# Head-by-head exponentials with bias and running sum in a decoder layer's self-attention softmax

## The chip, the cores and the metric

The kernel is one launch on one core of a Trainium2 chip. The metric is the device time of one execution in microseconds (us). All arithmetic is in 32-bit floats.

## The reference, cut to what matters

The reference is one decoder layer: each of three blocks (self-attention, cross-attention to a context, and a mixture-of-experts feed-forward) is applied to a layer-normed input and added to the residual. Only the first block is touched here. There are 8 sequences of 112 tokens, width 512, 16 heads of 128.

```python
k = jnp.einsum('ihd,bpd->biph', W_K, x)          # x is already layer-normed
q = jnp.einsum('ihd,bpd->biph', W_Q, x)
v = jnp.einsum('ihd,bpd->biph', W_V, x)
scores = jnp.einsum('biph,biqh->biqp', k, q)
mask = jnp.tril(jnp.ones((pos, pos), dtype=x.dtype))
masked = scores * mask - jnp.float32(10000000000.0) * (1.0 - mask)
attn = jax.nn.softmax(masked / jnp.sqrt(jnp.float32(d_head)), axis=-1)
z = jnp.einsum('biqp,biph->biqh', attn, v)
z_flat = jnp.transpose(z, (0, 2, 1, 3)).reshape(b, pos, -1)
out = jnp.einsum('df,bqf->bqd', W_O, z_flat)
```

The softmax needs, for each sequence, head and query, the largest score of the row, the exponentials of the scaled differences to it, their sum, and the division by that sum.

## The kernel before, in words

The 896 tokens lie in 7 tiles of 128 rows. Rows 0 to 111 of tile t hold sequence t+1; sequence 0 is cut into seven pieces of 16 tokens which fill rows 112 to 127 of all tiles. The program names this with `seq(ap, b)`.

Self-attention runs over four groups (`g`) of four heads each (`GH = 4`). A group has three stages.

1. **Queries and keys.** `pair_of_heads` makes `qT` and `kT` for the group, with a scheme of sums that saves matmuls (lines 249 to 282; TensorE line 261). GpSimd forms the weight sums.
2. **Softmax and values.** A loop over sequences 1, 0, 2, 3, 4 calls `softmax(b)` and then `value(i)`. `value(i)` (line 338) is eight matmuls for one token tile; ScalarE copies them out (line 342), and a DMA on SP's queue (line 343, `v<-v`) carries the 16 rows of sequence 0 into a tile of their own, `vals[0]`. Values 5 and 6 follow without a softmax.
3. **Weighted sums and output projection.** `turn(b)` transposes the softmax weights of four heads on TensorE (line 218) and ScalarE copies them to `sT` (line 220); `weighted(b)` multiplies them with the values (line 226) and VectorE copies the result to `zT` (line 233); `project_o(t)` multiplies `zT` with the output weights (line 348) and VectorE adds it to the residual (line 355). The remaining softmaxes 5, 6 and 7 are called in this loop, in iterations b = 1, 2 and 3, four sequences ahead of their use.

One call of `softmax(b)` works on four heads at once, a tile `s` of 112 rows by 4 x 112 scores. TensorE writes the scores to PSUM (line 191). VectorE adds the mask while it copies them to SBUF (line 199), takes the row maxima `mx` (line 206) and subtracts them (line 207). ScalarE takes the exponential of the whole tile in one instruction, with the factor 1/sqrt(128) as its scale (line 208). VectorE sums the rows to `sm` (line 210) and inverts the sums (line 211). GpSimd multiplies (line 212).

Four PSUM buffers, the pool `sc`, are shared in turn by the scores `s`, the transposes `pT` and the sums `z`: a new one waits until the one four allocations earlier has been read out. The tile framework orders the instructions of each engine when it builds the program, and puts in the waits; each engine then works its queue strictly in order. On TensorE the third stage of a group begins pT(1), pT(0), s(5), pT(2), z(1), s(6), pT(3), z(2), z(0), s(7), pT(4), z(3), where s(5) are the scores of sequence 5, pT(1) the transpose of sequence 1 and z(0) the weighted sum of sequence 0. The first projection, called o(0) below, comes next in the first three groups, and needs zT(0) and zT(1).

Of the kernel before, what the change touches and what calls it, by code (L numbers as in the profile page):

```python
# [17 lines left out]
AF = mybir.ActivationFunctionType  # L18
ALU = mybir.AluOpType
AX = mybir.AxisListType  # L20

P = 128
B, S, D = 8, 112, 512
# [5 lines left out]
H, DH = 16, 128  # L29
GH = 4  # L30
# [29 lines left out]
def seq(ap, b):  # L60

    if b:
        return ap[..., (b - 1) * P : (b - 1) * P + S]
    axes = " ".join("abcd"[: len(ap.shape) - 1])
    return ap.rearrange(f"{axes} (t i) -> {axes} t i", t=TT)[..., S:]


def like_seq(ap, b):

    if b:  # L70
        return ap
    axes = " ".join("abcd"[: len(ap.shape) - 1])
    return ap.rearrange(f"{axes} (t i) -> {axes} t i", t=TT)
# [3 lines left out]
def decoder_layer(  # L77
    ctx: ExitStack, tc: tile.TileContext, x, ctxT, wqk, wv_all, wo, wx, wgate, wsgu, wsd, wegu, wed_a, wed_b, consts, out
):
    nc = tc.nc  # L80
# [15 lines left out]
    mask = cst[:S, C_MASK : C_MASK + S]  # L96
# [20 lines left out]
    def psum(pool, name):  # L117
        return pool.tile([P, 512], F32, tag=pool.name, name=name)

    def load_w(pool, src, name):  # L120
        t = pool.tile([P, 4, 512], F32, tag="w", name=name)
        nc.sync.dma_start(out=t, in_=src)
        return t
# [53 lines left out]
    with ExitStack() as sa:  # L177
# [10 lines left out]
        def softmax(b, qT, kT, q0):  # L188
            ps = psum(sc, "s")
            for h in range(GH):  # L190
                nc.tensor.matmul(  # L191
                    like_seq(ps[:S, h * S : (h + 1) * S], b),
                    qT[:, h, (b - 1) * P : (b - 1) * P + S] if b else q0[:, h, :],
                    seq(kT[:, h, :], b),
                    start=True,
                    stop=True,
                )
            s = sp.tile([S, GH, S], F32, tag="s", name="s", bufs=5)
            nc.vector.tensor_tensor(
                s,  # L200
                ps[:S, : GH * S].rearrange("q (h p) -> q h p", h=GH),
                mask[:, None, :].to_broadcast([S, GH, S]),
                ALU.add,
            )
            mx = sp.tile([S, GH], F32, tag="mx", name="mx")
            nc.vector.tensor_reduce(mx, s, AX.X, ALU.max)
            nc.vector.tensor_tensor(s, s, mx[:, :, None].to_broadcast([S, GH, S]), ALU.subtract)  # L207
            nc.scalar.activation(s, s, AF.Exp, scale=float(DH) ** -0.5)  # L208
            sm = sp.tile([S, GH], F32, tag="sm", name="sm")
            nc.vector.tensor_reduce(sm, s, AX.X, ALU.add)  # L210
            nc.vector.reciprocal(sm, sm)  # L211
            nc.gpsimd.tensor_tensor(s, s, sm[:, :, None].to_broadcast([S, GH, S]), ALU.mult)  # L212
            return s
# [9 lines left out]
        def weighted(b, sT, v, zT):  # L223
            pz = psum(sc, "z")
            for h in range(GH):
                nc.tensor.matmul(  # L226
                    pz[:, h * S : (h + 1) * S],
                    v[:S, h * DH : (h + 1) * DH],
                    sT[:, h, :],
                    start=True,  # L230
                    stop=True,
                )
            nc.vector.tensor_copy(
                seq(zT, b), like_seq(pz[:, : GH * S].rearrange("p (h q) -> p h q", h=GH), b)
            )
# [48 lines left out]
        for g in range(NG):  # L284
            if g == 0:

                wq, wk = (wpool.tile([P, 4, 512], F32, tag="w", name=f"w{i}_0") for i in range(2))
                for h in range(GH):
                    for i, w in enumerate((wq, wk)):
                        nc.sync.dma_start(out=w[:, h, :], in_=wqk[i, g][:, h, :])  # L290
            else:
                wq, wk = (load_w(wpool, wqk[i, g], f"w{i}_{g}") for i in range(2))
            wv = load_w(wvpool, wv_all[g], f"w2_{g}")
            wog = wvpool.tile([P, 4, 512], F32, tag="w", name=f"wo_{g}")
            load = nc.sync.dma_start(out=wog, in_=wo[g])
            if g == 0:
                first_weights = load.ins
                with tc.issue_after(first_weights):
                    nc.sync.dma_start(out=gw, in_=wgate)
                    nc.sync.dma_start(  # L300
                        out=slots.rearrange("(j p) d -> p j d", p=P),
                        in_=zeros[:, None, :].to_broadcast([P, NS, D]),
                    )
            qT = qkp.tile([P, GH, NT], F32, tag="qT", name="qT")
            kT = qkp.tile([P, GH, NT], F32, tag="kT", name="kT")
            zT = zp.tile([P, GH, NT], F32, tag="zT", name="zT")
            for h in range(0, GH, 2):
                for w, dst, pool in ((wq, qT, mm), (wk, kT, sc)):
                    if g == 0 and h == 0 and dst is qT:

                        for half in range(2):
                            cols = bass.ds(half * HALF, HALF)
                            for i in range(2):
                                ps = psum(mm, "qk")
                                for c in range(ND):
                                    nc.tensor.matmul(
                                        ps[:, :HALF],
                                        w[:, i, c * P : (c + 1) * P],
                                        xn1[:, c, cols],
                                        start=(c == 0),  # L320
                                        stop=(c == ND - 1),
                                    )
                                nc.scalar.copy(dst[:, i, cols], ps[:, :HALF])
                            if half == 0:
                                rs1 = norm1(4, TT)
                                for t in range(4, TT):
                                    ln_apply(mv1, rs1[t - 4], t, xn1)
                                token_sums()
                        continue
                    pair_of_heads(w, h, dst, pool)  # L330
            soft, turned, vals = {}, {}, {}
            vals[0] = v0p.tile([S, GH * DH], F32, tag="v0", name="v0")

            def value(t):

                ps = psum(mm, "v")
                for c in range(ND):
                    nc.tensor.matmul(  # L338
                        ps, xn1[:, c, t * P : (t + 1) * P], wv[:, c, :], start=(c == 0), stop=(c == ND - 1)
                    )  # L340
                vals[t + 1] = vp.tile([P, GH * DH], F32, tag="v", name="v")
                nc.scalar.copy(vals[t + 1], ps)
                nc.sync.dma_start(out=vals[0][t * SP : (t + 1) * SP, :], in_=vals[t + 1][S:, :])

            def project_o(t):
                ps = psum(mm, "o")
                for h in range(GH):
                    nc.tensor.matmul(  # L348
                        ps,
                        zT[:, h, t * P : (t + 1) * P],  # L350
                        wog[:, h, :],
                        start=(h == 0),
                        stop=(h == GH - 1),
                    )
                nc.vector.tensor_tensor(xs[t], ps, xs[t], ALU.add)  # L355
                if g == NG - 1:
                    ln_stats(mv2, t)


            q0 = vp.tile([P, GH, S], F32, tag="q0", name="q0", bufs=1)  # L360
            nc.gpsimd.tensor_copy(like_seq(q0, 0), seq(qT, 0))
            for i, b in enumerate((1, 0, 2, 3, 4)):
                soft[b] = softmax(b, qT, kT, q0)
                value(i)
            for i in (5, 6):
                value(i)
            for b in (1, 0):
                turned[b] = turn(soft.pop(b))
            for b in range(1, B):
                if b + 4 < B:  # L370
                    soft[b + 4] = softmax(b + 4, qT, kT, q0)
                if b + 1 < B:
                    turned[b + 1] = turn(soft.pop(b + 1))
                weighted(b, turned.pop(b), vals.pop(b), zT)
                if b == 2:
                    weighted(0, turned.pop(0), vals.pop(0), zT)
                elif b > 2:
                    project_o(b - 3)
            project_o(TT - 2)
            project_o(TT - 1)  # L380
# [347 lines left out]
    with ExitStack() as ff:  # L728
# [335 lines left out]
        h = {}  # L1064
# [109 lines left out]
```

## Time and profile before

| what | value |
|---|---|
| median of 3 runs | 1017.53 us (1015.96 to 1018.1) |
| the profiled execution's own time | 1016.08 us |
| its span, first to last instruction | 1014.3 us |
| TensorE's granted clock | 1.00 |
| busy: TensorE matmul, VectorE, ScalarE, GpSimd | 98%, 40%, 27%, 25% of the span |
| self-attention, four groups | about 14 to 448 us of the span |
| cross-attention; feed-forward | to about 760 us; to the end |

A busy share is the time in which an engine had an instruction under way. In the views, PE is TensorE's matmul, PEld its weight load, DVE is VectorE, ACT is ScalarE, POOL is GpSimd, SP the engine that issues most DMAs. An arrow `s<-qT,kT` names the tile written and the tiles read. Brackets in the timeline give the idle time of the engine before an instruction and what ended it; that name is inferred from semaphore events, and where an instruction has several waits it is the one that came last by the profile.

### The profile page before, as it was taken

Reading aid. Unit: us, or ns where it says so; the run is one execution under the profiler, and the core shown is the slowest. Engines: PE = TensorE matmul, PEld = TensorE weight load, DVE = VectorE, ACT = ScalarE, POOL = GpSimd, SP = SyncE. Lnnn points to the kernel's source line nnn. Section 1 sums busy time; section 2 is a strip of 40 time slices with the busy share of each in tenths; the row PEclk is TensorE's granted clock in tenths of the full one; section 3 lists DMA queues with packets and bytes.
Section 4 is the critical chain, followed back from the end, with each engine's and each line's share of the span. In section 5 each row is a group of like instructions: output and inputs, shape, how many; then the busy total and the mean of one; then the engine's idle time right before and its main releaser. Section 6 shows DMA issues by size and latency. Waiting matters only on the chain.

```text
span 1014.3 us, 14761 instructions
## 1 busy us (share of the span) xinstructions
PE 991.4 (98%) x5732; PEld 527.0 (52%) x5732; DVE 401.9 (40%) x769; ACT 276.9 (27%) x522; POOL 246.6 (24%) x269
## 2 busy tenths in 40 slices
PE   5999999999999999999999999999999999999998
PEld 3556555654556455645455555565565544444433
DVE  4345224532345225545432444343425333333315
ACT  2122011310022012213354555455543111221100
POOL 4341034103411122112533223330205600000023
PEclk9999999999999999999999999999999999999999
DMA  9521002101201111000000001000209738777765
GB/s 343 201 83 47 5 38 84 50 1 42 79 16 41 42 41 47 5 1 0 31 32 1 32 32 32 2 32 2 83 3 377 297 112 258 235 235 236 216 190 171
DMA packets 31093, 95.66 MB, mean 94 GB/s; under 512 B 3888, under 2 KB 5808, under 8 KB 27440
## 3 DMA queue, kind: packets, MB, share of 16 engines
q1 hardware_dynamic: 25968, 82.11, 24.0%
q0 software_dynamic: 2320, 7.63, 2.3%
q10 hardware_dynamic: 2736, 4.98, 1.6%
q8 instruction: 46, 0.75, 0.3%
q14 instruction: 23, 0.19, 0.1%
HBM read 78.85 MB, written 14.94 MB: 92 GB/s over the span
## 4 chain that ended last, share of the span: by engine, by line
PE 90%; issue 3%; DVE 3%; DMA 2%; POOL 1%; ACT 1%; SPq 0%; DVEq 0%; POOLq 0%; ACTq 0%
PE qk L261 16%; PE o L348 10%; PE v L338 10%; PE kv L482 9%; PE gu L744 5%; PE xs L577 5%; PE gate L980 4%; PE y L1002 4%; PE up L980 4%; PE pv L602 4%; PE ys L1028 3%; PE k L423 3%; PE xv L423 3%; PE z L226 2%; PE s L191 2%
## 5 line engine op out<-in xcount | busy, mean ns | idle before, releaser
L585 ACT ACTIVATE e<-xs 125x448 f32<-125x448 f32 x192 | 88.4, 545 | 72.7 <-PE xs L577 72.7
L338 PE MATMUL v<-w,xn 128*128 128x512 f32 x224 | 100.4, 594 | 0.0
L348 PE MATMUL o<-wo,zT 128*128 128x512 f32 x224 | 99.8, 594 | 0.0
L261 PE MATMUL qk<-xc,wc 128*128 128x448 f32 x180 | 70.1, 539 | 0.0
L348 PEld LDWEIGHTS o<-wo,zT 128*128 128x128 f32 x224 | 41.0, 190 | 44.0 <-issue 44.0
L338 PEld LDWEIGHTS v<-w,xn 128*128 128x128 f32 x224 | 40.7, 190 | 42.1 <-issue 41.1
L212 POOL TENSOR_TENSOR s<-s,sm 112x448 f32<-112x448 f32 x32 | 30.1, 941 | 129.2 <-DVE sm L211 100.5
L1013 POOL DMA_INDIRECT got<-routed,at x14 | 14.7, 1054 | 173.4 <-DMA routed<-y 169.1
L980 PE MATMUL gate<-wex,xT 128*64 x144 | 55.3, 466 | 0.5 <-ACT xT L945 0.5
L744 PE MATMUL gu<-xn,sw 128*128 128x448 f32 x144 | 55.5, 541 | 0.0
L980 PE MATMUL up<-wex,xT 128*64 x144 | 54.3, 459 | 0.0
L577 PE MATMUL xs<-qT,kT 32*125 32x224 f32 x768 | 50.4, 373 | 1.5 <-DVE qT L540 1.5
L930 DVE COPY xn<-wex 128x704 f32 x60 | 31.2, 524 | 51.5 <-PE up L980 51.5
L261 PEld LDWEIGHTS qk<-xc,wc 128*128 128x128 f32 x180 | 34.2, 190 | 33.4 <-issue 32.3
L261 PE MATMUL qk<-xn,w 128*128 128x448 f32 x120 | 50.2, 539 | 0.0
L577 PEld LDWEIGHTS xs<-qT,kT 32*125 32x125 f32 x768 | 33.2, 181 | 32.5 <-issue 28.5
L1002 PE MATMUL y<-wd,hT 128*64 128x512 f32 (+1 forms) x216 | 49.5, 593 | 0.6 <-ACT y L1006 0.6
L980 PE MATMUL gate<-xn,xT 128*64 128x352 f32 x120 | 45.9, 464 | 0.0
L980 PE MATMUL up<-xn,xT 128*64 128x352 f32 x120 | 45.3, 459 | 0.0
L355 DVE TENSOR_TENSOR x<-o,x 128x512 f32<-128x512 f32 x28 | 19.3, 688 | 62.2 <-PE o L348 62.2
L271 ACT COPY p<-qk 128x448 f32<-128x448 f32 x15 | 8.0, 532 | 126.7 <-PE qk L261 126.7
L208 ACT ACTIVATE s<-s 112x448 f32<-112x448 f32 x32 | 18.5, 577 | 84.3 <-DVE s L207 78.9
(211 smaller groups left out, 1665.4 us busy)
## 6 DMA issues: line engine op xcount, KB each, us to landing
wd<-in_wed_a SPq DMA_DIRECT2D x27, 512.0 KB, 3.8
wex<-in_wegu SPq DMA_DIRECT2D x8, 1408.0 KB, 19.9
wd<-in_wed_b SPq DMA_DIRECT2D x36, 192.0 KB, 4.6
w<-in_wqk SPq DMA_DIRECT2D x6, 1024.0 KB, 4.7
ctx<-in_ctxT SPq DMA_DIRECT2D x8, 750.0 KB, 9.0
slots<-zeros SPq DMA_DIRECT2D x1, 4608.0 KB
wd<-in_wed_a SPq DMA_DIRECT2D x18, 256.0 KB, 4.3
routed<-y SPq DMA_DIRECT2D x18, 256.0 KB, 3.4
```

What stands on the lines that cost most here:

```text
L261: nc.tensor.matmul(ps[:, :HALF], wt[:, c * P : (c + 1) * P], x[:, c, :], start=(c == 0), stop=(c == 1))
L338: nc.tensor.matmul(ps, xn1[:, c, t * P : (t + 1) * P], wv[:, c, :], start=(c == 0), stop=(c == ND - 1))
L348: nc.tensor.matmul(ps, zT[:, h, t * P : (t + 1) * P], wog[:, h, :], start=(h == 0), stop=(h == GH - 1),)
L423: nc.tensor.matmul(ps[:MC, :], ctxs[b][:, c, m * MC : (m + 1) * MC], w[:, c, :], start=(c == 0), stop=(c == ND - 1),)
L482: nc.tensor.matmul(ps[:MC, :], x[:, c, :], w[:, c, :], start=(c == 0), stop=(c == 1))
L577: nc.tensor.matmul(strips[j][:MC, ci * 2 * S : (ci + 1) * 2 * S], keys[b][rows, 2 * cp + ci, m * MC : (m + 1) * MC], queries[b][rows, 2 * ...
L585: last_exp[(b, cp, m)] = nc.scalar.activation(e[:, :, j, :, :].rearrange("p c e s -> p c (e s)"), strips[j][:MC, : 4 * S].rearrange("p (c ...
L602: nc.tensor.matmul(ps[VW * j : VW * (j + 1), g * S : (g + 1) * S], v[:, m, 16 * cp + h, :], es[m][:, h // 8, (h % 8) // 2, h % 2, :], star ...
L744: nc.tensor.matmul(ps[:, :HALF], w[:, c, i % 2, k, :], xn3[:, c, cols], start=(c == 0), stop=(c == ND - 1))
L930: nc.vector.tensor_copy(second(j, c), wex[:, bass.ds(moved[j], 1), c, :].rearrange("p o f -> p (o f)"))
L980: nc.tensor.matmul(gu[k][n, :FF], xT[:, c, n], w, start=(c == 0), stop=(c == ND - 1))
L1002: nc.tensor.matmul(ps[n, :], hT[:fn, i, n], w[i][:fn], start=(i == 0), stop=(i == len(FCH) - 1))
```

## The change

The mask is added and the scale applied in one VectorE instruction. The maximum is taken negated, so that it can serve as the bias of ScalarE's exponential. The subtraction and the sum on VectorE are gone. In place of one exponential over 112 x 448 there are four over 112 x 112, each with its head's column of `mx` as bias and with its row sum written to its head's column of `sm`. The inversion and the multiplication move into a function of their own, `normalise`, which is called one step later in the program: after `value(i)` in the first loop and after `weighted(b)` in the second.

```diff
             s = sp.tile([S, GH, S], F32, tag="s", name="s", bufs=5)
-            nc.vector.tensor_tensor(
-                s,
-                ps[:S, : GH * S].rearrange("q (h p) -> q h p", h=GH),
-                mask[:, None, :].to_broadcast([S, GH, S]),
-                ALU.add,
+            nc.vector.scalar_tensor_tensor(
+                out=s,
+                in0=ps[:S, : GH * S].rearrange("q (h p) -> q h p", h=GH),
+                scalar=float(DH) ** -0.5,
+                in1=mask[:, None, :].to_broadcast([S, GH, S]),
+                op0=ALU.mult,
+                op1=ALU.add,
             )
             mx = sp.tile([S, GH], F32, tag="mx", name="mx")
-            nc.vector.tensor_reduce(mx, s, AX.X, ALU.max)
-            nc.vector.tensor_tensor(s, s, mx[:, :, None].to_broadcast([S, GH, S]), ALU.subtract)
-            nc.scalar.activation(s, s, AF.Exp, scale=float(DH) ** -0.5)
+            nc.vector.tensor_reduce(mx, s, AX.X, ALU.max, negate=True)
             sm = sp.tile([S, GH], F32, tag="sm", name="sm")
-            nc.vector.tensor_reduce(sm, s, AX.X, ALU.add)
+            for h in range(GH):
+                nc.scalar.activation(s[:, h, :], s[:, h, :], AF.Exp, bias=mx[:, h : h + 1], accum_out=sm[:, h : h + 1])
+            return s, sm
+
+        def normalise(s, sm):
             nc.vector.reciprocal(sm, sm)
             nc.gpsimd.tensor_tensor(s, s, sm[:, :, None].to_broadcast([S, GH, S]), ALU.mult)
             return s
...
             for i, b in enumerate((1, 0, 2, 3, 4)):
-                soft[b] = softmax(b, qT, kT, q0)
+                weights = softmax(b, qT, kT, q0)
                 value(i)
+                soft[b] = normalise(*weights)
...
             for b in range(1, B):
                 if b + 4 < B:
-                    soft[b + 4] = softmax(b + 4, qT, kT, q0)
+                    weights = softmax(b + 4, qT, kT, q0)
                 if b + 1 < B:
                     turned[b + 1] = turn(soft.pop(b + 1))
                 weighted(b, turned.pop(b), vals.pop(b), zT)
+                if b + 4 < B:
+                    soft[b + 4] = normalise(*weights)
```

In the changed program the copies, the projection and the inversion stand a few lines lower than in the kernel before: the exponential is line 211, the inversion 215, the copy of `sT` 224, the copy of `zT` 237, the projection 352.

## The prediction

> **What bounds the kernel now.** I read the page's busy shares first, then the stages one by one, then the timeline of one stage. On the page:
>
> ```profile
> PE 991.4 (98%) x5732; PEld 527.0 (52%) x5732; DVE 401.9 (40%) x769; ACT 276.9 (27%) x522; POOL 246.6 (24%) x269
> PE 90%; issue 3%; DVE 3%; DMA 2%; POOL 1%; ACT 1%; SPq 0%; DVEq 0%; POOLq 0%; ACTq 0%
> ```
>
> TensorE is busy 98% of the span and carries 90% of the chain that ended last. An average may hide a stage with another limit, so the second view is the busy time of each engine in the four stretches with softmax, values and projection:
>
> ```profile
> 78.00:126.00 48.00, 47.50 (x202) 27.87 (x201) 18.99 (x35) 8.02 (x15) 3.77 (x5) 1.00 0.08 25
> 168.00:233.00 65.00, 64.57 (x268) 37.35 (x268) 29.59 (x55) 12.66 (x23) 9.43 (x11) 1.00 0.12 36
> 276.00:341.00 65.00, 64.22 (x267) 37.06 (x266) 29.72 (x55) 12.66 (x23) 9.01 (x11) 1.00 0.11 37
> 383.00:448.00 65.00, 64.95 (x272) 37.67 (x271) 35.65 (x71) 14.25 (x25) 7.46 (x8) 1.00 0.07 20
> ```
>
> The columns are the stretch, its length, then PE, PEld, DVE, ACT and POOL. PE is idle 0.50, 0.43, 0.78 and 0.05 us: 1.76 us in all four groups. That is the ceiling of what an easier softmax can give back here. The timeline of the second group shows where the idle lies:
>
> ```profile
> 195.39 0.93 PE L218 MATMUL pT<-cst,s 112*112 112x112 f32 x8
> 196.20 0.51 SPq L343 DMA_DIRECT2D v<-v  x1
> 197.81 0.62 DVE L206 TENSOR_REDUCE mx<-s 112x4 f32<-112x448 f32 x1
> 199.65 0.53 ACT L220 COPY sT<-pT 112x448 f32<-112x448 f32 x1 [1.59 <-PE pT L218]
> 200.88 1.12 PE L226 MATMUL z<-sT,v 112*128 112x112 f32 x8 [0.43 <-DVE mx L206]
> 203.22 0.61 DVE L233 COPY zT<-z 128x448 f32<-128x448 f32 x1
> 203.90 3.69 PE L348 MATMUL o<-wo,zT 128*128 128x512 f32 x8
> ```
>
> All 0.43 us lie before z(0), at 200.88. The bracket names VectorE's maximum, but z(0) doesn't read it, and the PSUM buffer that z(0) takes was freed by the copy of zT(1) at 199.05. What z(0) does need is `vals[0]`, whose last piece SP issues at 196.20, 4.68 us earlier. In the first group the same instruction waits 0.50 us and the bracket says DMA v<-v, issued 4.74 us before; in the third 0.78 us, again DMA, 5.03 us. In the fourth there is no such wait: the median landing of this DMA is 1.9 us, and only in the first three groups does a load of the next value weights leave 0.6 us ahead of it. So **the idle belongs to a transfer**, and the softmax is hidden behind TensorE nearly everywhere.
>
> **What the Trainium skill says.** "VectorE: DVE Perf Modes", on the TRN2 errata, gives an fp32 tensor_tensor (N+151)/0.96 ns: 624 at N=448. The rows below agree (620, 622). "ScalarE: Activation LUTs", on what ACT_TABLE_LOAD costs, gives an ACTIVATE with a pointer as bias 280 + 0.833 N ns, 93 less with an immediate, and lets neighbours overlap by 93 ns. At N=32 and 96 that is 307 and 360; the trace has 321 and 372. Two copies of 0.535 us in a row take 0.97, an overlap of 0.10. "ScalarE activation tables", on what a function is, says that the accumulator adds up results along the free dimension; it has no price for reading it out, and no row of the trace before shows it.
>
> **The change part by part.** Prices, from the groups by shape (busy us, mean ns):
>
> ```profile
> L207 DVE TENSOR_TENSOR s<-s,mx 112x448 f32<-112x448 f32 x32 | 19.9, 622 | 0.8
> L199 DVE TENSOR_TENSOR s<-s,cst 112x448 f32<-112x448 f32 x32 | 19.8, 620 | 48.0 <-PE s L191 48.0
> L210 DVE TENSOR_REDUCE sm<-s 112x4 f32<-112x448 f32 x32 | 19.8, 620 | 16.5 <-ACT s L208 16.5
> L208 ACT ACTIVATE s<-s 112x448 f32<-112x448 f32 x32 | 18.5, 577 | 84.3 <-DVE s L207 78.9 <-DVE sm L211 5.4
> L417 ACT ACTIVATE kss<-kss,eps_rms 125x96 f32<-125x96 f32 x8 | 3.0, 372 | 1.3 <-DVE kss L413 1.2
> L417 ACT ACTIVATE qss<-qss,eps_rms 128x32 f32<-128x32 f32 x7 | 2.2, 321 | 7.4 <-DVE qss L413 7.4
> L713 ACT ACTIVATE warm<-eps_rms 1x1 f32<-1x1 f32 x7 | 1.4, 202 | 0.1
> ```
>
> *VectorE.* The subtraction and the sum go: 19.9 + 19.8 = 39.7 us less. The scaled mask is a scalar_tensor_tensor; at 128x512 that form takes 751 ns (line 1019) where a tensor_tensor takes 688 (line 355), so 0 to 63 ns more each, at most 2.0 us. The negated maximum costs what the maximum does. Net 38 to 40 us, all of it beside TensorE's work: worth 0 on the path but for the places below.
>
> *ScalarE.* 18.5 us go and 128 small exponentials come. Call d the time from the start of one to that of the next. Between the two L417 rows, 112 elements with a bias take 0.385 us; less the overlap, 0.29. That is the floor, if reading the sum is free. The ceiling is a separate instruction of 0.30 us (line 147, three elements with a bias, 298 ns) and no overlap: 0.68. I take 0.45, a read of the size of the 202 ns row, partly overlapped. ScalarE then gains 128 x 0.45 - 18.5 = 39 us and is busy about 31% of the span.
>
> *First loop, per sequence.* TensorE takes 4.24 us. VectorE would end mask and maximum 1.3 us after it starts, ScalarE the exponentials 4d = 1.8 later and the copy of v after them: 2.4 of 4.24 us. The inversion, which now waits in VectorE's queue ahead of the next mask, is through some 0.9 us before that is due. Hidden up to d of about 0.68. The v<-v transfers follow ScalarE's copies; the last two copies have no exponential ahead of them, so the transfer that z(0) waits for starts when it did. No DMA moves on SP's queue, and GpSimd's queue keeps its order.
>
> *Third stage, where cover is thin.* As built, TensorE's queue is the same in three groups; ScalarE's runs exp(5) x4, sT(3), exp(6) x4, sT(4), exp(7) x4; VectorE's runs inversion(5), zT(2), inversion(6), zT(0), mask(7). So zT(0), which o(0) needs, now stands behind an inversion that waits for eight small exponentials. In the second group: maximum(5) ends at 198.43, exponentials start at 198.5; 4d; sT(3) 0.53 less 0.09; 4d: the last leaves its slot at 198.94 + 8d, and about 0.1 passes until it has ended; inversion and copy, 0.17 + 0.61 overlapped, bring zT(0) to **199.8 + 8d**. At d = 0.45 that is 203.4, against 203.83 before and o(0) at 203.90: no loss. The break is at d = 0.51; in the first and third group at 0.52 and 0.55, since their o(0) comes later behind the longer DMA wait. sT(3) ends at 198.5 + 4d + 0.5 = 200.8; the transpose that takes its PSUM buffer starts at 202.62: hidden. Inversion(7) waits to about 206.6, ahead of the residual's addition at 207.67: hidden. The weights of sequences 5, 6 and 7 are multiplied by 201.4, 203.7 and 207.7; their transposes come at 207.43, 212.16 and 216.88.
>
> *Fourth group.* There VectorE's queue has zT(0) ahead of inversion(6): no loss. z(3) waited 0.27 us in its weight load for zT(2), which comes 0.9 us sooner: 0.1 us gained on the matmuls.
>
> *Elsewhere* the order of work is the same: 0. **Sum:** -0.1 us against the profiled execution's 1016.08 (span 1014.3), with -1.8 (all idle recovered) and +3.7 (d = 0.68: 1.30 + 1.36 + 1.02) as ends. That execution stands 1.45 us below the median of the three runs; against the median I forecast no change, 1017.5.
>
> **The rivals.**
> *ScalarE late (slower).* If d passes 0.51, zT(0) holds o(0) back at 8 us per us of d in each of three groups: at 0.57 about 1 us in all, at 0.61 about 2, at 0.68 3.7, time 1021.2. For it: the read of the sum is unpriced and paid 32 x 4 times. Against it: overlap is seen on this engine wherever instructions stand back to back. Chance 0.18 beyond 0.2%.
> *VectorE was the wait (faster).* If the bracket at 200.88 is right, all of 1.76 us comes back: 1015.8. For it, the words "DVE mx" in the bracket; against it, the first and third group's DMA and the missing wait in the fourth. Even then it stays inside 0.2%, so faster by more than that, 0.09, needs a gain that I don't see.
> *The change doesn't unload what it says*, for instance since the framework reorders the queues: the built queues show fewer VectorE instructions and the same TensorE order but for one swap in the fourth group, where o(0) now precedes pT(5): no time either way.
>
> **How the numbers follow.** 0.2% is 2.0 us, about what a measurement of this kernel can tell from no change; the three runs alone differ by 2.1. No change within it: 0.73. The range goes from 1015.5 (all idle back, and 0.2) to 1021.2 (d at its ceiling).
>
> **What would show it.** Right: PE's idle in the four stretches is again near 0.5, 0.4, 0.8 and 0; VectorE is some 39 us less busy; the small exponentials start under 0.5 us apart; o(0) directly follows z(3). Wrong: an idle before o(0) released by zT, longer as d grows, or an idle before z(0) that is gone.

## The result, and the profile after

Median of 22 runs each, in turn on one chip: **1016.75 us after** (1014.65 to 1020.27) against 1018.72 before, a ratio of **0.9977**, 95% interval 0.9966 to 0.9987. The profiled execution after took 1017.38 us, its span 1015.6. A repeat of both kernels (first experiment) gave 0.9992, interval 0.9982 to 1.0001. The gain is small: about 0.6 to 1.0 us between executions of the same kind, of which the profiles locate 0.6. The rest of the 2 us between the first two medians isn't the softmax's, as the sizes below show.

The page of the kernel after, first the busy shares and then the engines' shares of the chain of waits:

```profile
PE 993.0 (98%) x5732; PEld 528.1 (52%) x5732; DVE 364.1 (36%) x705; ACT 309.0 (30%) x746; POOL 246.8 (24%) x269
PE 91%; issue 3%; DVE 2%; DMA 2%; POOL 1%; ACT 1%; SPq 0%; DVEq 0%; POOLq 0%; ACTq 0%
```

VectorE is 37.8 us less busy (401.9 to 364.1), ScalarE 32.1 more (276.9 to 309.0), TensorE 1.6 more (a slower start, see the experiments). The busy time in the same four stretches (length, then PE, PEld, DVE, ACT, POOL, clock, DMA share, GB/s):

```profile
78.00:126.00 48.00, 47.59 (x209) 28.31 (x208) 14.55 (x27) 13.23 (x48) 4.66 (x5) 1.00 0.08 25
168.00:233.00 65.00, 64.62 (x274) 37.60 (x273) 21.30 (x40) 20.68 (x79) 11.37 (x13) 1.00 0.11 37
276.00:341.00 65.00, 64.27 (x272) 37.53 (x271) 20.98 (x40) 20.70 (x79) 11.09 (x13) 1.00 0.11 37
383.00:448.00 65.00, 65.00 (x274) 37.84 (x273) 27.02 (x55) 22.26 (x81) 7.83 (x9) 1.00 0.07 20
```

PE is idle 0.41, 0.38, 0.73 and 0.00 us, 1.52 in all, where it was 1.76: nearly all of the idle has stayed. The groups by shape (busy us, mean ns, idle ahead and its releaser) give the prices that were unknown:

```profile
L211 ACT ACTIVATE s<-s,mx 112x112 f32<-112x112 f32 x128 | 48.0, 376 | 60.3 <-DVE mx L208 60.0
L211 ACT ACTIVATION_READ_ACCUMULATOR s<-s,mx 112x1 f32 x128 | 23.9, 187 | 0.0
L199 DVE SCALAR_TENSOR_TENSOR s<-s,cst 112x448 f32<-112x448 f32 x32 | 20.0, 624 | 55.0 <-PE s L191 55.0
```

Each small exponential of 376 ns brings an instruction of its own, 187 ns, that reads the running sum out. The scaled mask costs what the mask did, 624 against 620. The second group in the timeline, which stands 2.02 us later on this execution's clock than in the timeline shown of before:

```profile
197.61 0.33 SPq L122 DMA_DIRECT2D w<-in_wv  x1
198.22 0.51 SPq L347 DMA_DIRECT2D v<-v  x1
...
200.93 0.37 ACT L211 ACTIVATE s<-s,mx 112x112 f32<-112x112 f32 x1
...
201.21 0.19 ACT L211 ACTIVATION_READ_ACCUMULATOR s<-s,mx 112x1 f32 x1
...
201.30 0.37 ACT L211 ACTIVATE s<-s,mx 112x112 f32<-112x112 f32 x1
...
202.85 1.12 PE L230 MATMUL z<-sT,v 112*128 112x112 f32 x8 [0.38 <-DVE sm L215]
204.40 0.59 DVE L237 COPY zT<-z 128x448 f32<-128x448 f32 x1
205.87 3.61 PE L352 MATMUL o<-wo,zT 128*128 128x512 f32 x8
```

The read starts 0.28 us after its exponential and the next exponential 0.09 after the read: d, from one start to the next, is **0.37 us**. zT(0) is ready at 204.99, 202.97 on the clock of before; the formula 199.8 + 8d gives 202.8. o(0) starts 0.9 us later and waits for nothing. z(0), at 202.85, still waits 0.38 us. The bracket named the maximum before and names the inversion now. z(0) reads neither.

### The profile page after: what moved, and what is told of

The parts are those of the page before. It is cut to its first block, busy times and chain, and to the rows that moved or that the text cites. A ratio compares the mean times of both kernels' runs of the same rounds, so it can differ in the third digit from the quotient of the medians.

```text
span 1015.6 us, 14915 instructions
## 1 busy us (share of the span) xinstructions
PE 993.0 (98%) x5732; PEld 528.1 (52%) x5732; DVE 364.1 (36%) x705; ACT 309.0 (30%) x746; POOL 246.8 (24%) x269
## 4 chain that ended last, share of the span: by engine, by line
PE 91%; issue 3%; DVE 2%; DMA 2%; POOL 1%; ACT 1%; SPq 0%; DVEq 0%; POOLq 0%; ACTq 0%
PE qk L265 16%; PE v L342 10%; PE o L352 9%; PE kv L489 9%; PE gu L751 5%; PE xs L584 5%; PE gate L987 4%; PE y L1009 4%; PE up L987 4%; PE pv L609 4%; PE ys L1035 3%; PE k L430 3%; PE xv L430 3%; PE z L230 3%; PE s L191 2%
## 5 line engine op out<-in xcount | busy, mean ns | idle before, releaser
L211 ACT ACTIVATE s<-s,mx 112x112 f32<-112x112 f32 x128 | 48.0, 376 | 60.3 <-DVE mx L208 60.0
L359 DVE TENSOR_TENSOR x<-o,x 128x512 f32<-128x512 f32 x28 | 19.4, 692 | 68.6 <-PE o L352 68.6
```

Of the source, the lines that this page charges most:

```text
L211: nc.scalar.activation(s[:, h, :], s[:, h, :], AF.Exp, bias=mx[:, h : h + 1], accum_out=sm[:, h : h + 1])
```

## The experiments

The theory: all of the idle in the first three groups belongs to the v<-v transfer, so a lighter softmax can't show there. The rivals: VectorE is the wait, as the bracket says; or a wait for VectorE stands just behind the transfer and appears when that is gone.

**Both kernels again**, with no edit.

`c1_before`:

> The kernel before, unchanged, timed against itself: what a ratio is worth. If the spread of the times lies in the start (TensorE at half pace for a longer or shorter stretch of the first matmuls, 2.1 us between the two profiles at hand), the ratio may miss 1 by up to 0.1% either way and the times fall into groups some 2.5 us apart. If the runs before were taken on a fair footing and the whole 0.23% is the change, it stays within 0.05% of 1.

`c1_after`:

> The changed kernel again. By stage, the two profiles at hand differ by 0.6 us in self-attention and 0.3 us ahead of the routed experts, 0.9 us in all, or a ratio of 0.9991. If that is the change, the ratio falls between 0.998 and 1.000 and, between groups of times with the same start, the difference is 0.7 to 1.0 us. If the change is worth 2.3 us, the ratio is 0.9977 again and the profile shows 2 us somewhere behind the start.

The kernel before gave 1018.37 beside itself (ratio 1.0009, 0.9994 to 1.0023), the one after 1016.43 (0.9992, 0.9982 to 1.0001; median of before in this series 1017.25). Times of one kernel fall in groups 2 to 3.5 us apart. In this series before has 24 of 67 runs around 1015.44, 35 around 1017.40 and 8 around 1020.74; after has 4 around 1014.44 and 18 around 1016.46, so it is **0.9 to 1.0 us** faster within a group. In the first comparison, before has 2, 13 and 7 runs at 1015.82, 1018.27 and 1020.99, after has 10, 10 and 2 at 1015.19, 1017.56 and 1020.09: 0.6 to 0.9 us within a group, the rest of the 2 us from the mix.

Two things make the groups. In the highest one TensorE's mean clock reads 0.996 or 0.997 (12 of the 67 executions, 8 in that group and 4 in the middle one); a stretch that does this is shown in the last section. The two lower groups differ in TensorE's pace at the start. The timeline of its weight loads in the first projection, in the profiled execution of before:

```profile
14.83 0.19 PEld L316 LDWEIGHTS qk<-xn,w 128*128 128x128 f32 x1 [0.19 <-issue]
```

and in that of after, with one from the time when full pace was reached:

```profile
15.51 0.33 PEld L320 LDWEIGHTS qk<-xn,w 128*128 128x128 f32 x1 [0.41 <-issue]
...
19.82 0.19 PEld L320 LDWEIGHTS qk<-xn,w 128*128 128x128 f32 x1 [0.19 <-issue]
```

Loads stand 0.375 us apart in before from the beginning, 0.75 in after until 19.4 us; the first 16 matmuls take 6.28 against 8.39 us. That makes up the 2.02 us by which the second group is late, and it depends on the execution: the repeated before has the slow start too, 8.40 us. So I compare stages from here on. Attention, from the third projection of the first group to the next block, is 425.01 and 424.76 us in the two profiles of before and 424.42 and 424.17 in those of after: **0.6 us less in both pairs**. A third pair, the two kernels with early matmuls below, has 425.15 and 424.88, only 0.27 less. What all three pairs share is the fourth group: from its first scores to the end of its projections 65.06 us in before (65.07 in the third pair) and 64.73 in after (64.74). The same stretches of the first three groups add up to 196.65, 196.39 and 196.78 us in before and to 196.39, 196.13 and 196.84 in after; no difference is shown there.

The third group's z(0) in the repeat of after, in the timeline, names the transfer:

```profile
309.88 1.12 PE L230 MATMUL z<-sT,v 112*128 112x112 f32 x8 [0.56 <-DMA v<-v]
```

**The next value weights issued behind the last v<-v.** This takes away what the transfer waits behind, in both kernels:

```diff
-            wv = load_w(wvpool, wv_all[g], f"w2_{g}")
+            if g == 0:
+                wv = load_w(wvpool, wv_all[g], f"w2_{g}")
+            else:
+                with tc.issue_after(last_v):
+                    wv = load_w(wvpool, wv_all[g], f"w2_{g}")
...
-                nc.sync.dma_start(out=vals[0][t * SP : (t + 1) * SP, :], in_=vals[t + 1][S:, :])
+                return nc.sync.dma_start(out=vals[0][t * SP : (t + 1) * SP, :], in_=vals[t + 1][S:, :]).ins
...
-                value(i)
+                last_v = value(i)
```

`c1_after_defer`:

> The changed kernel with the next group's value weights issued behind the last v<-v transfer of the group, on the same queue. If the idle before z(0) is that transfer's, its landing falls from about 4.6 to about 2 us, the idle before z(0) goes in all three groups, and PE gains 0.41 + 0.38 + 0.73 = 1.5 us against the changed kernel. If VectorE or ScalarE holds z(0), the idle stays and nothing is gained.

`c1_before_defer`:

> The kernel before with the same move of the value weights. If the idle before z(0) is the transfer's in the old softmax too: 0.50 + 0.43 + 0.78 = 1.7 us less, though where VectorE is later with its copies (zT for the transpose's PSUM buffer and for o(0)) a part comes back, as in the fourth group, where z(3) waited 0.27 us: so 1.0 to 1.7 us. If the bracket at 200.88 was right and VectorE's maximum was the wait, 0.

After became 1014.53 (ratio to before 0.9977, 0.9966 to 0.9988), before 1016.13 (0.9982, 0.9973 to 0.9991). Of after's 22 executions 9 have the lower mean clock, of before's none, so these medians understate the distance. The timeline of after with the deferred load, second group:

```profile
196.71 0.51 SPq L351 DMA_DIRECT2D v<-v  x1
...
197.31 0.53 SPq L122 DMA_DIRECT2D w<-in_wv  x1
...
199.90 1.95 PE L230 MATMUL z<-sT,v 112*128 112x112 f32 x16
```

The weights now leave 0.6 us after the transfer, not before it, and z(0) runs in one piece with the sum ahead of it: it starts halfway through the 1.95 us, near 200.9, with no wait. Where the trace tells when the group's last v<-v landed, that was 4.4 to 4.6 us after its issue in the two profiles of after, and it is 1.9 us with the deferred load. The softmax, VectorE's work and TensorE's order are untouched, so **the wait was the transfer's**. The busy time of the second group's stretch, first before, then after, both with the deferred load:

```profile
168.00:240.00 72.00, 71.95 (x291) 41.17 (x290) 31.92 (x58) 13.73 (x25) 11.57 (x14) 1.00 0.14 47
```

```profile
168.00:240.00 72.00, 72.00 (x293) 41.31 (x292) 22.76 (x42) 21.75 (x81) 10.56 (x13) 1.00 0.14 48
```

Attention took 422.24 us in after and 423.56 in before: 1.3 us apart, where the two kernels were 0.6 apart with the transfer in the way. The deferred load gave after 1.9 to 2.2 us there, more than the 1.5 us expected from its idle, and before 1.2 to 1.5, as expected. A wait costs more than the idle shown: sums in an unbroken row overlap a little. In the second group of after, z(0) starts 0.54 us later behind z(1) than with the deferred load, where the bracket has 0.38, and takes 1.12 us instead of 1.06. What is left in before with the deferred load, in its waits and its timeline:

```profile
PEld z L226 <- DVE zT L233: 1.1, 4, 0.3
```

```profile
204.52 0.97 PEld L226 LDWEIGHTS z<-sT,v 112*128 112x128 f32 x8 [0.27 <-DVE zT L233]
```

z(3) waits in its weight load for VectorE's copy zT(2), 0.27 us, once in each of the four groups. The kernel before has that wait in the fourth group only. After with the deferred load hasn't got it: its four groups take 64.73 us each, against 65.06. z(3) starts 0.21 us sooner, and 0.09 that before spends between its first two matmuls goes too. In before, the deferred load also moved pT(5) ahead of o(0) in TensorE's queue, as in its fourth group; the last 0.03 may be that. So the second rival holds beside the theory: **the transfer hid a wait for VectorE**, which the changed softmax takes away.

The repeat of before shows the same without any edit. In its first group the transfer came early, and z(0) was held for 0.12 us only. Then o(0) waited for zT:

```profile
98.00 0.30 PEld L348 LDWEIGHTS o<-wo,zT 128*128 128x128 f32 x2 [0.32 <-DVE zT L233]
```

The group's softmax and projection took 65.47 us, no less than the 65.46 of the first profile, where z(0) was held for 0.50.

**VectorE's two passes put back**, on top of the deferred load, into a spare tile that nobody reads:

```diff
+            mx2 = sp.tile([S, GH], F32, tag="mx2", name="mx2")
+            nc.vector.tensor_reduce(mx2, s, AX.X, ALU.max)
             for h in range(GH):
...
+            nc.vector.tensor_reduce(mx2, s, AX.X, ALU.add)
             return s, sm
```

`c2_defer_vpad`:

> The changed kernel with the deferred load, and the two VectorE passes put back that the change took out: a reduction of the scores ahead of the exponentials and one behind them, into a spare tile (0.62 us each, 64 in all). If the change gains by VectorE's time where the transposes' buffers and o(0) wait for the copies of zT, then most of the 1.3 us between the two kernels with deferred load (self-attention from the second block of qk to the last o: 406.29 and 404.96 us) comes back. If it gains by the moved inversion or by the split exponentials, the stretch stays at 405.0.

1015.55 us (0.9975, 0.9966 to 0.9984; before 1017.81 in this series). Attention went from 422.24 to 423.04 us: 0.8 of the 1.3 came back, and so did the wait, in the view of the waits:

```profile
PEld z L233 <- DVE zT L240: 0.7, 4, 0.2
```

So most of the 1.3 us is VectorE's time. Of the other 0.5 some 0.4 is that wait again, which is 0.1 us shorter in each group than in before with the deferred load (0.7 against 1.1 us over the four). The passes stood at other places in VectorE's queue than the old ones, and the inversion stayed where the change had moved it; which of the two does this wasn't tried.

**Early matmuls**: 28 multiplications of a constant tile into a PSUM tile that nobody reads, ahead of the first transposes, so that TensorE is at full pace when the first projection comes.

```diff
+    warm = psum(mm, "warm")
+    for i in range(28):
+        nc.tensor.matmul(warm[:, :P], ones, ones, start=True, stop=True)
```

`c2_before_warm`:

> The kernel before with 28 matmuls of the constant ones ahead of the first transposes, their result unused. TensorE is idle until 9.85 us and then takes its first ten projections at half pace (0.75 us between weight loads in place of 0.375) in some executions and not in others. If the spread of times is that start, the early matmuls bring the full pace forward in every execution: the groups of times 2.4 us apart become one, at or up to 2 us below the lowest group of before (1015.0 to 1015.8). If the spread comes from elsewhere, the times stay spread and the median stays near 1017.3.

`c2_after_warm`:

> The changed kernel with the same 28 matmuls. With the start out of the way its distance from the kernel before with them is the change alone: 0.9 us by the stages of the profiles (0.6 in self-attention, 0.3 ahead of the routed experts); 2.3 us if the first measured ratio was the change, 0 if the stage differences were chance.

`c2_after_defer_warm`:

> The changed kernel with the value weights behind the last v<-v transfer and the 28 matmuls. If the two gains lie in different stages they add: 2.0 us below the changed kernel with the matmuls alone, and the fastest of all. If the earlier gain of the deferred load came from the start, less than 1 us.

| kernel with early matmuls | median us | ratio to before (interval) | main group |
|---|---|---|---|
| before | 1015.59 | 0.9985 (0.9976 to 0.9995) | 17 of 22 around 1015.48 |
| after | 1015.08 | 0.9981 (0.9970 to 0.9991) | 16 of 22 around 1014.90 |
| after, deferred load | 1012.28 | 0.9947 (0.9930 to 0.9964) | all 6, 1012.24 to 1012.77 |

From the first projection to the third, the start takes 8.18 to 8.48 us in the profiles of these three and 8.42 to 10.65 in the others. Against my expectation the times didn't become one group: the 5 and 6 executions outside the main groups all have a mean clock of 0.996 to 0.998, so the early matmuls take away the spread of the start and not the other one. With the start settled, the changed kernel is **0.58 us** faster, 1015.48 - 1014.90, less than the 0.9 that I had expected. The last row is the fastest kernel of this study: its median is 5.5 us or 0.53% below that of before, and 3.6 us below the lowest group of before in this series (1015.90). It is 2.6 us below the main group of after with early matmuls, where I had expected 2.0.

**One and two more exponentials for each head**, into a spare tile and without the sum, to put the break to the test. The order of the queues is held by hand (the copies of zT behind the last inversion, the transposes' copies behind the exponentials named), with the aim that only d changes:

```diff
+                nc.scalar.activation(spare, s[:, h, :], AF.Exp, bias=mx[:, h : h + 1])
                 nc.scalar.activation(s[:, h, :], s[:, h, :], AF.Exp, bias=mx[:, h : h + 1], accum_out=sm[:, h : h + 1])
...
+            with tc.issue_after(inversions[-1]):
                 nc.vector.tensor_copy(
```

(the second kernel has the added line twice).

`c3_exp_twice`:

> The changed kernel with one more exponential per head, into a spare tile and without a sum, and with the queue orders of the changed kernel's first three groups kept in all four (sT(3) behind exp(5), zT(0) behind inversion(6)). The step from head to head grows from 0.37 us by the price of an exponential without the read, 0.28 us, to d = 0.65. By the prediction's formula zT(0) then ends at 199.8 + 8d = 205.0 on the clock of the second group of before, 1.1 us after o(0) could start: self-attention gets longer by about 1.1 + 1.1 + 0.8 us in three groups and 1.7 us in the fourth, 4 to 5 us in all. If ScalarE is hidden whatever it does, 0.

`c3_exp_thrice`:

> The same with two more exponentials per head: d = 0.93. The formula adds 8 x 0.28 = 2.2 us to each of the four groups against one more exponential: 13 to 14 us over the changed kernel. If the loss is not a queue of eight exponentials ahead of o(0) but a fixed wait, it stays near that of one more exponential.

*One more*: 1025.38 us, ratio 1.0072 (1.0050 to 1.0095). d was 0.79, not the 0.65 expected. From first projection to last, the four groups took 3.50, 1.84, 1.48 and 2.44 us more than after's, 9.3 in all where 4 to 5 were expected. For d = 0.79 the formula gives 2.2 in the second group and 1.9 in the third, 0.4 above the measurement in each. In the first, part of the 3.50 is something else. Its stretch, and four microseconds of it:

```profile
78.00:126.00 48.00, 46.20 (x200) 27.43 (x199) 13.85 (x26) 19.79 (x68) 4.66 (x5) 0.96 0.07 25
```

```profile
102.00:106.00 4.00, 4.00 (x9) 1.76 (x8) 0.18 (x1) 1.46 (x6) 0.93 (x1) 0.71 0.00 0
```

PE is idle 1.80 us, 1.39 more than after, and after that wait the granted clock falls to 0.71: 4% of 48 us, another 1.9 by estimate, is lost to the clock. And the wait isn't where the formula put it. In the timeline:

```profile
211.33 0.47 PE L236 MATMUL z<-sT,v 112*128 112x112 f32 x2 [1.52 <-ACT sT L230]
```

It is z(4), waiting for ScalarE's copy of the transpose of sequence 4, which stands behind the exponentials of sequence 6. As built, this kernel's TensorE queue had the first two matmuls of that sum ahead of o(0), so TensorE's order had changed beside d. That ScalarE becomes late as d grows is shown; that it does so through zT(0) and o(0) isn't, and the near agreement in size is no proof of that path.

*Two more*: 1053.12 us, ratio 1.0351 (1.0316 to 1.0387), 36 us over after where 13 to 14 were expected, far past the 8 us per us of d. The busy time by four microseconds in the second group:

```profile
216.00:220.00 4.00, 0.36 (x4) 0.14 (x2) 0.62 (x3) 3.84 (x14) 0.30 (x1) 0.88 0.01 2
220.00:224.00 4.00, 3.97 (x6) 1.94 (x7) 0.60 (x2) 3.71 (x14) 0.64 (x1) 0.50 0.02 4
```

ScalarE is busy 3.84 of 4 us while TensorE does next to nothing, and afterwards TensorE works at a clock of 0.50. Over the four stretches PE is idle 21.5 us, and the clock below 1.00 there is worth, by estimate, another 14 us: less the 1.5 of idle that after has anyway, that is 34 of the 35 us by which attention is longer in this profile. With d near 1.2, four heads' exponentials alone, 4.8 us, pass the 4.24 us that TensorE takes for a sequence in the first loop. That the backlog from there lands on the third stage fits, but wasn't tried by itself.

## Why the prediction was right, and where it was off

- *What bounds it.* Right. TensorE carries 91% of the chain, the idle again reads 0.41, 0.38, 0.73 and 0, and o(0) directly follows z(3). The deferred load showed the one contested point, that the idle ahead of z(0) is the transfer's. The rival "VectorE was the wait" fails as it was put: z(0) still waits with a VectorE that has 38 us less to do. But a wait for VectorE stood close behind it, which the prediction took for hidden though its lines have zT(0) ready only 0.07 us before o(0). "Doesn't unload" fails by the busy shares. The 1.76 us of idle was no ceiling: the fourth group shows 0.05 of it and gave back 0.33.
- *VectorE.* Forecast 38 to 40 us less, measured 37.8. The scaled mask cost at most 2.0 us by forecast, and 32 x 4 ns = 0.1 in fact. Added up one by one, VectorE's instructions are 40.0 us shorter; 2.2 us of that had overlapped other VectorE instructions, which the busy time counts once.
- *ScalarE and d.* Taken 0.45 between 0.29 and 0.68; measured 0.37. The read is an instruction of 187 ns, near the 202 ns that I likened it to, but all but 0.09 us of it lies beside others. The 0.385 us at 112 elements was read "between" rows of 32 and 96 elements, yet lies beyond them; the row now there has 0.376. ScalarE's 39 us more came out as 32.1, its share as 30%. For the price of an exponential, the Trainium skill, "ScalarE: Activation LUTs", on what ACT_TABLE_LOAD costs, has 280 + 0.833 N ns, an estimate of 373 at N = 112, and the row has 376. The section has no price for the read.
- *ScalarE late.* The break at 0.51 wasn't reached, and zT(0) was ready 0.2 us from where the formula has it. Beyond the break, ScalarE does turn late, but the kernel with one more exponential found another wait first.
- *Fourth group, -0.1 us.* Mis-sized: -0.33, in each of the three pairs of profiles. z(3)'s wait for zT(2) goes; it cost 0.21 us to the start of z(3), where the prediction had 0.1, and 0.09 behind that. The swap of o(0) and pT(5) is within the 0.03 that is left, as the prediction had it. z(3)'s weight load in the timeline of before, then z(3) and o(0) in that of after, without a wait:

```profile
417.94 0.97 PEld L226 LDWEIGHTS z<-sT,v 112*128 112x128 f32 x8 [0.27 <-DVE zT L233]
```

```profile
419.59 1.06 PE L230 MATMUL z<-sT,v 112*128 112x112 f32 x8
...
420.48 3.61 PE L352 MATMUL o<-wo,zT 128*128 128x512 f32 x8
```

- *First three groups, 0.* Held as far as these profiles tell: together -0.26, -0.26 and +0.06 us in the three pairs, while one kernel's sum differs by up to 0.7 from profile to profile.
- *Elsewhere, 0.* Wrong by 0.28 us. The stretch ahead of the routed experts is 64.70 us with the old softmax and 64.42 in every profile with the changed one. In it an ACT_TABLE_LOAD starts earlier: its two waits end 0.3 us apart in before and together in after, with the same program order. What moves the table load, I haven't found; it wasn't tried.

The sum that every pair of profiles shows is -0.33 - 0.28, about -0.6 us, against -0.1 forecast. The first comparison's 0.23% lies just outside the 0.2% that the forecast called no change, with an interval from 0.13 to 0.34%; the repeat's 0.08% lies inside. The first value was raised by the mix of starts and clocks, which the prediction didn't foresee. So the forecast was right by its mechanism, and in size by a narrow margin.

## What to carry to other kernels

A bracket names the releaser seen last; before believing it, ask what the instruction reads, and where a transfer feeds it, look at what was issued ahead of that on its queue. A wait that ends last hides the one that ends just before it, so the same change was worth 0.3 to 0.6 us of attention with the transfer in place and 1.3 without: take away the masking wait, then judge. Small instructions that went one by one to a half-idle engine were free here only up to a break: work it out per item from that engine's queue, as an average share (30% here) doesn't show it.

## What the runs showed of the hardware that I had not expected

- The sum of ScalarE's exponential is no free by-product: 187 ns as an instruction of its own for each head, 0.09 us of the step when another follows. Spare and real exponentials in turn overlapped less: two in 0.79 us. The real one overwrites in place what the spare one reads, which may be the reason; it wasn't tried.
- TensorE starts at half pace in some executions of the same program and not in others, 2 us apart, while the views' clock reads 1.00 there: the trace's record of the clock begins only at 13.2 us in before, at 18.9 in after, and at 4.4 to 4.8 in the three kernels with early matmuls. With these, the first 16 matmuls took 6.28 us in all three profiles.
- The clock can also fall in mid-kernel. In the repeat of before it was 0.50 for 6.8 us, from 701.1 on, behind a wait of 1.07 us, as its timeline and its busy time there show:

```profile
699.97 1.09 PE L160 MATMUL ln_t<-cst,xn 128*128 128x128 f32 x8 [1.07 <-DVE v L505]
```

```profile
702.00:706.00 4.00, 4.00 (x31) 3.07 (x34) 0.00 (x0) 1.96 (x4) 0.00 (x0) 0.50 0.02 4
```

That block, cross-attention, took 3.2 us more than in the other profiles of before. But in the first of these the same instruction waits 1.07 us too, and the clock stays at 1.00. So the wait alone doesn't decide it, and what does, these runs don't show. With one more exponential the clock was 0.50 for 3.4 us behind the first group's wait of 1.52 us, and not behind the same wait in the other groups.
